# A state-space layer and a mixture of experts on one core: four states' products by TensorE in every sequence, and experts begun beside their second sequence's dispatch

## The chip, the cores and the metric

The kernel runs on one core of one Trainium2 chip. The metric is device time in microseconds (us) of one execution; lower is better. The engines have their usual names: TensorE (PE in the profile, with its weight loads as PEld), VectorE (DVE), ScalarE (ACT), GpSimd (POOL) and SyncE (SP), which here only issues DMAs.

## The reference

The input is 16 sequences of 512 positions and 256 channels, in float32. Two layers follow each other, each with a residual and a layer norm.

The first is a bidirectional selective state-space layer. A sequence is projected to 512 inner channels, convolved and gated. For each direction, with `u` (the convolved input), a step width `dt` per channel and position, and `B`, `C` per state and position (16 states), it computes

```
dA     = dt * A                                  # A negative, per channel and state
dB_u   = dt * u * B
dA_cum = exp(sum of dA over the later positions)
xs     = cumsum(dB_u * dA_cum) / (dA_cum + 1e-12)
y      = sum over states of xs * C  +  u * D
```

The two directions are added, gated and projected back to 256 channels.

The second is a soft mixture of 16 experts with 64 slots each. Logits of every position against 1024 slot embeddings are turned by a softmax over the positions into *dispatch* weights and by a softmax over the slots into *combine* weights. Each slot is the dispatch-weighted sum of a sequence's positions. Each expert applies `gelu(slots @ Wg + bg) * (slots @ Wu + bu) @ Wd + bd` to its slots, and the combine weights bring the results back to the positions.

## The kernel before

**The scan.** Sequences `b` = 0 to 15 run one after the other. A sequence has four parts (`scan_part`): direction `r` = 0 or 1, and half `p` of the channels (two blocks of 128 channels each). A part has 16 steps: for each pair of states `n, n+1` and each of the two blocks `c` there is one step, so a sequence has 64 steps and the kernel 1024. A step does, for the two states `j` = 0 and 1 of its block:

- GpSimd multiplies `du = dt * u` with the broadcast rows of `B`: `db` (L442), 128x1024 for both states.
- ScalarE computes the decay `exp(A * dt)` (L459), written into the PSUM tile `h`, and `th`, a tanh (L461) that stands for the division by `dA_cum + 1e-12`.
- VectorE runs the recurrence `h = h * decay + db` along the positions (L465 forward, L467 backward), and multiplies `(th + 1) * h` into `hg` (L470).
- GpSimd multiplies `hg` with the broadcast rows of `C` (L471).
- TensorE adds `hg` up over the states in the PSUM tile `acc` (L386, eight transposing matmuls). This is issued two steps later (`add_up(2)`).

For some states, TensorE makes `dt*u*B` in place of GpSimd (`by_diagonal`, L420): four matmuls of the transposed `du` (`duT`, L364) with a matrix that holds `B` on its diagonals (`dg`, loaded from DRAM) write the product into a PSUM tile `hd`. The step's `db` then has one state only (128x512), the decay of the other state goes into an SBUF tile `dec`, and the scan runs in place in `hd`. Which states is told by `diag_of`: 3, 7, 11 and 15 in sequences 0 to 2, and 5 and 13 from sequence 3 on. The matmuls for a step are issued after the step before it.

**PSUM.** Tiles `h` rotate through a pool of three banks (`ps_h`), `acc` through two, and everything else on TensorE through three shared banks (`bank()`, pool `ps`). In the kernel before, `hd` is one of the users of the shared banks. `diags` holds the number of each `hd` that is still waiting for its scan, so that no other user runs it over.

**What lies beside the scan.** Three lists of generators (`Side`) supply other work piece by piece. After each scan step, `beside_scan` calls on all of them:

- `prep`: the projections for the next part (`prep_forward`, `turn_back`, `prep_pair`, `turn_pair`), one piece per step.
- `front`: `finish` of the sequence before (transposes `pyt`, projection `po` L651, norm, `px2`) and its `dispatch` (logits `pl` L710, transposes `pd` L731, slots `pq` L746). Its 32 pieces are paced over the 64 steps.
- `back`: `experts` for a pair of sequences, in eight pairs of experts, each with the matmuls `pg` (L869, with the bias by L864), `pu` (L811) and `peo` (L838); and `combine` for each of the two sequences, with `cl` (L933), `ctp` (L954) and `cpo` (L1015) for each of four row blocks.

A piece ends with the matmuls into its banks; what reads the banks is issued at a later step (`HOLD`). A piece is begun only where the banks suffice. `paced_piece` gives a list its pieces: each step adds (pieces left) / (steps left) to a credit, and a piece takes 1.0 from it. Since all engines run their instructions in order, a piece on TensorE delays the `acc` and `hd` behind it, and a reader of it on VectorE or ScalarE delays the scans.

Experts of the sequences 2g and 2g+1 are put into `back` at the start of sequence 2g+3, when the dispatch of both is over, and with the two combines are spread over 128 steps, that is over an odd and the next even sequence. In effect the experts lie in the odd sequence and the combines in the even one. In the last sequence all that is left has 64 steps (`hurry`), and pieces marked `GAP` are no longer held off by a step. Experts and combine of the last two sequences follow after the scan, with more banks and buffers.

Of the kernel before, what the change touches and what calls it, by code (L numbers as in the profile page):

```python
# [9 lines left out]
F32 = mybir.dt.float32  # L10
# [7 lines left out]
P = 128  # L18
L = 512
# [36 lines left out]
def seq_layers(tc, ident, neghalf, a, out):  # L56
# [21 lines left out]
    nb = a["x"].shape[0]  # L78
    with ExitStack() as ctx:
# [17 lines left out]
        ps_h = scan_psum.enter_context(tc.tile_pool(name="m_h", bufs=3, space=PSUM))  # L97
# [7 lines left out]
        count = [0]  # L105

        def bank(name):
            count[0] += 1
            if tail and count[0] % 8 >= 3:
                return tail[0].tile([P, 512], F32, tag="tps", name=name)  # L110
            return ps.tile([P, 512], F32, tag="mps", name=name)
# [167 lines left out]

        def diag_of(b):  # L280

            return (3, 7, 11, 15) if b < 3 else (5, 13)

        def project_unit(b, r, out):

# [121 lines left out]
        def scan_part(b, r, p, v, accs, done, then):  # L407

            prep.drain()
            prep.gens += [[1, g] for g in [turn_pair(b, r, p, v)] + then]  # L410
            w, ds = side[r], diag_of(b)
            made = {}

            def by_diagonal(n, c):

                diags.append(count[0])
                made[n, c] = h = bank(f"hd_{b}_{r}_{n}_{c}")
                for lc in range(NL):
                    s = slice(lc * P, (lc + 1) * P)
                    ins = nc.tensor.matmul(h[:, s], v[c][3][:, s], dg[:, s], start=True, stop=True)  # L420
                    if lc == 0:
                        late(ins)

            chunks = (2 * p, 2 * p + 1)
            for n in range(0, NS, 2):
                q = f"{b}_{r}_{p}_{n}"
                k = 1 if n + 1 in ds else 2
# [11 lines left out]
                for c in chunks:  # L439
# [7 lines left out]
                    for j in range(2):  # L447
# [3 lines left out]
                        else:  # L451
                            h = made.pop((n + j, c))
# [4 lines left out]
                    for j in range(2) if k == 2 else (1, 0):  # L457
# [1 line left out]
                        nc.scalar.activation(hs[j][1], dt, AF.Exp, scale=w["A"][:, c, s])  # L459
                        ths[j] = p4.tile([P, L], F32, tag="th", name=f"th_{q}_{c}_{j}")  # L460
                        nc.scalar.activation(ths[j], rr, AF.Tanh, bias=LN_1E12 / 2, scale=w["Ah"][:, c, s])  # L461
                    for j in range(2):
                        (h, dec, add), th = hs[j], ths[j]
                        if r == 0:
                            nc.vector.tensor_tensor_scan(h, dec, add, 0.0, ALU.mult, ALU.add)  # L465
                        else:
                            nc.vector.tensor_tensor_scan(  # L467
                                h[:, ::-1], dec[:, ::-1], add[:, ::-1], 0.0, ALU.mult, ALU.add
                            )
                        nc.vector.scalar_tensor_tensor(hg[:, j, :], th, 1.0, h, ALU.add, ALU.mult)  # L470
# [5 lines left out]

                    nxt_n = n if c == chunks[0] else n + 2
                    if nxt_n + 1 in ds:
                        for x in sides:
                            x.take_up()  # L480
                        by_diagonal(nxt_n + 1, chunks[1] if c == chunks[0] else chunks[0])
                    beside_scan()
                    if k == 1:
                        diags.pop(0)
                    add_up(2)

        class Side:


            def __init__(self):  # L490
                self.gens, self.hold, self.need, self.left, self.credit = [], None, 0, 0, 0.0
                self.wait = self.took = self.gap = False

            def add(self, steps, gen):
                self.gens.append([steps, gen])

            def begin(self, scan_steps):
                self.left, self.credit = scan_steps, 0.0
# [20 lines left out]
            def piece(self, gaps=True):  # L519

                done = False
                while self.gens and self.hold is None and not self.wait:
                    if self.gap and self.took and gaps:
                        break
                    oldest = min([x.hold for x in sides if x.hold is not None] + diags[:1], default=count[0])
                    if count[0] - oldest + self.need > BANKS:
                        break
                    done = True
                    head = self.gens[0]
                    head[0] = max(head[0] - 1, 1)  # L530
                    fresh = len(head) == 2
                    if fresh:
                        head.append(True)
                    self.go()
                    if not fresh and (not self.gens or self.gens[0] is head):
                        break
                return done

            def paced_piece(self, gaps):
                self.credit = min(self.credit + sum(x[0] for x in self.gens) / max(self.left, 1), 2.0)  # L540
                self.left -= 1
                if self.credit >= 1.0 and self.piece(gaps):
                    self.credit -= 1.0

            def drain(self):
                while self.gens:
# [2 lines left out]
                    self.piece()  # L549

        hurry = False
        diags = []

        prep, front, back = sides = [Side(), Side(), Side()]

# [479 lines left out]
                yield WAIT  # L1035
                put(0, NL, *both)

        FINISH, COMBINE, PAIR = 32, 14, 4
        fwd = {}
        prep.add(1, prep_forward(0, 0, ND, fwd))  # L1040
        prep.drain()
# [6 lines left out]
        for b in range(nb):  # L1048
            bwd, nxt, accs = {}, {}, {}

            if b >= 3 and b % 2 == 1:
                g = (b - 3) // 2
                back.add(8 * PAIR, experts(g, 0, 8))
                back.add(COMBINE, combine(2 * g))
                back.add(COMBINE, combine(2 * g + 1))
            hurry = b + 1 == nb
            front.begin(64)
            back.begin(128 if b % 2 == 1 and b + 1 < nb else 64)

            def gate(c, b=b, accs=accs, bwd=bwd):  # L1060
                y = bwd["res"]
# [32 lines left out]
        g, kept = nb // 2 - 1, {}  # L1094
# [52 lines left out]
```

## Time and profile before

| What | us |
|---|---|
| median of three runs | 5326.35 (5323.48 to 5327.91) |
| the profiled execution | 5322.25 |
| its span in the profile | 5320.5 |
| sequence 2 (four states by TensorE, no back work) | 284.5 |
| sequence 3 (two states, experts) | 321.5 |
| sequence 8 (two states, combine) | 308.6 |
| sequence 9 (two states, experts) | 326.9 |
| sequence 14 (two states, combine) | 308.8 |
| sequence 15 (two states, experts and combine) | 372.6 |
| from the last scan step to the end | 240 |

A sequence is cut here at the end of every 64th product of L471. Sequences 4, 6, 10, 12 are within 1 us of sequence 8, and sequences 5, 7, 11, 13 within 1 us of sequence 9.

In a line of a group, the profile gives line, engine, operation, output<-inputs, shapes and count; then the busy time and the mean duration of one in ns; then the engine's idle time just before such instructions and what ended most of it. TensorE works on float32 here: one matmul of the program shows as two records in the profile, and a transposing one as one. In a line of a stretch the numbers after the length are the busy times of PE, PEld, DVE, ACT and POOL with their instruction counts, then the TensorE clock that was granted (1 is full), the DMA share and GB/s. In a line of waits: who waited for whom, total us, how often, the longest.

### The profile page before, as it was taken

Reading aid. Unit: us, or ns where it says so; the run is one execution under the profiler, and the core shown is the slowest. Engines: PE = TensorE matmul, PEld = TensorE weight load, DVE = VectorE, ACT = ScalarE, POOL = GpSimd, SP = SyncE. Lnnn points to the kernel's source line nnn. Section 1 sums busy time; section 2 is a strip of 40 time slices with the busy share of each in tenths; the row PEclk is TensorE's granted clock in tenths of the full one; section 3 lists DMA queues with packets and bytes.
Section 4 is the critical chain, followed back from the end, with each engine's and each line's share of the span. In section 5 each row is a group of like instructions: output and inputs, shape, how many; then the busy total and the mean of one; then the engine's idle time right before and its main releaser. Section 6 shows DMA issues by size and latency. Waiting matters only on the chain. (4 is left out here: it accounts for less than half of the span.)

```text
span 5320.5 us, 74550 instructions
## 1 busy us (share of the span) xinstructions
PE 4310.4 (81%) x24498; PEld 3411.1 (64%) x24498; DVE 4560.6 (86%) x6284; ACT 4104.9 (77%) x6573; POOL 4681.6 (88%) x2537
## 2 busy tenths in 40 slices
PE   5677776897778978788788878889787897878889
PEld 3556565676567756676666766667666676657667
DVE  7999999889998899888898888988898889987733
ACT  6777878887888877888887887888778887777644
POOL 6999999989999899999999989998999989988710
PEclk7778888998899989999899988899888998889999
DMA  5444444675446644576446754467544664447545
GB/s 141 137 129 152 126 142 131 211 234 152 146 146 224 222 144 143 171 226 206 132 140 198 236 169 151 134 210 230 157 151 144 217 227 149 144 153 230 168 135 168
DMA packets 614820, 907.82 MB, mean 171 GB/s; under 512 B 84606, under 2 KB 404734, under 8 KB 614432
## 3 DMA queue, kind: packets, MB, share of 16 engines
q1 hardware_dynamic: 532740, 859.35, 50.9%
q10 hardware_dynamic: 81692, 43.70, 3.1%
q8 instruction: 195, 3.19, 0.2%
q14 instruction: 193, 1.58, 0.1%
HBM read 840.34 MB, written 62.56 MB: 170 GB/s over the span
## 5 line engine op out<-in xcount | busy, mean ns | idle before, releaser
L471 POOL TENSOR_TENSOR hg<-hg,cs 128x1024 f32<-128x1024 f32 x1024 | 2416.9, 2364 | 125.0 <-DVE hg L470 108.0
L442 POOL TENSOR_TENSOR db<-du,bs 128x1024 f32<-128x1024 f32 (+1 forms) x1024 | 2087.7, 2042 | 227.8 <-DVE h L465 84.1
L470 DVE SCALAR_TENSOR_TENSOR hg<-th,h 128x512 f32<-128x512 f32 x1744 | 1156.8, 679 | 183.4 <-PE acc L386 105.9
L386 PE MATMUL acc<-ident,hg 128*128 128x128 f32 x8192 | 1163.6, 292 | 106.4 <-POOL hg L471 84.6
L386 PEld LDWEIGHTS acc<-ident,hg 128*128 128x128 f32 x8192 | 1034.4, 152 | 284.6 <-POOL hg L471 131.3
L467 DVE TENSOR_TENSOR_SCAN h<-h,db 128x512 f32<-128x512 f32 x872 | 1044.9, 1219 | 104.9 <-ACT h L459 92.6
L465 DVE TENSOR_TENSOR_SCAN h<-h,db 128x512 f32<-128x512 f32 x872 | 1044.1, 1219 | 44.5 <-ACT h L459 43.6
L461 ACT ACTIVATE th<-rr,Ah_f 128x512 f32<-128x512 f32 x1024 | 724.6, 714 | 200.9 <-DVE hg L470 198.1
L461 ACT ACTIVATE th<-rr,Ah_b 128x512 f32<-128x512 f32 x1024 | 721.3, 712 | 153.5 <-DVE hg L470 143.5
L459 ACT ACTIVATE h<-dt,A_f 128x512 f32<-128x512 f32 x872 | 591.4, 680 | 99.5 <-DVE hg L470 96.3
L459 ACT ACTIVATE h<-dt,A_b 128x512 f32<-128x512 f32 x872 | 592.3, 680 | 85.6 <-DVE hg L470 81.7
L420 PE MATMUL hd<-dg,duT 128*128 128x128 f32 x2432 | 375.7, 305 | 73.2 <-ACT duT L364 27.1
L420 PEld LDWEIGHTS hd<-dg,duT 128*128 128x128 f32 x2432 | 347.9, 220 | 84.5 <-ACT duT L364 29.5
L710 PE MATMUL pl<-x2T,seT 128*128 128x512 f32 x512 | 294.1, 704 | 78.4 <-DVE hg L470 37.4
L838 PE MATMUL peo<-Wd,ht 128*128 128x256 f32 x1024 | 258.1, 408 | 63.2 <-DVE rr L346 36.6
L869 PEld LDWEIGHTS pg<-st,Wg 128*128 128x128 f32 x2048 | 243.1, 195 | 94.1 <-issue 82.8
L811 PE MATMUL pu<-st,Wu 128*128 128x128 f32 x2048 | 255.6, 284 | 49.3 <-DMA Wu<-in_Wu_dram 27.0
L1015 PE MATMUL cpo<-ceo,ct 128*128 128x256 f32 x1024 | 256.0, 407 | 43.2 <-DVE rr L346 40.0
L811 PEld LDWEIGHTS pu<-st,Wu 128*128 128x128 f32 x2048 | 245.9, 199 | 60.6 <-DVE h L467 29.5
L838 PEld LDWEIGHTS peo<-Wd,ht 128*128 128x128 f32 x1024 | 205.5, 206 | 106.1 <-DVE rr L346 39.2
L869 PE MATMUL pg<-st,Wg 128*128 128x128 f32 x2048 | 265.0, 284 | 4.5 <-DMA st<-s_dram 3.4
L1015 PEld LDWEIGHTS cpo<-ceo,ct 128*128 128x128 f32 x1024 | 207.2, 207 | 87.2 <-DVE rr L346 42.7
(165 smaller groups left out, 6754.0 us busy)
## 6 DMA issues: line engine op xcount, KB each, us to landing
cs<-bc SPq DMA_DIRECT2D x512, 512.0 KB, 3.9
bs<-bc SPq DMA_DIRECT2D x360, 512.0 KB, 5.2
Wg<-in_Wg_dram SPq DMA_DIRECT2D x128, 512.0 KB, 5.7
Wu<-in_Wu_dram SPq DMA_DIRECT2D x128, 512.0 KB, 5.8
Wd<-in_Wd_dram SPq DMA_DIRECT2D x128, 512.0 KB, 5.5
dg<-diag_dram SPq DMA_DIRECT2D x152, 256.0 KB, 4.3
bs<-bc SPq DMA_DIRECT2D x152, 256.0 KB, 3.5
x<-in_x_dram SPq DMA_DIRECT2D x32, 512.0 KB, 6.5
```

The costliest lines, as they stand in the source:

```text
L386: ins = nc.tensor.matmul(accs[c][:, s], hc[:, j, s], ident, is_transpose=True, start=False, stop=(last and j == 1 and lc == NL - 1),)
L420: ins = nc.tensor.matmul(h[:, s], v[c][3][:, s], dg[:, s], start=True, stop=True)
L442: nc.gpsimd.tensor_tensor(db[:, :k, :], du.unsqueeze(1).to_broadcast([P, k, L]), bs[:, :k, :], ALU.mult)
L459: nc.scalar.activation(hs[j][1], dt, AF.Exp, scale=w["A"][:, c, s])
L461: nc.scalar.activation(ths[j], rr, AF.Tanh, bias=LN_1E12 / 2, scale=w["Ah"][:, c, s])
L465: nc.vector.tensor_tensor_scan(h, dec, add, 0.0, ALU.mult, ALU.add)
L467: nc.vector.tensor_tensor_scan(h[:, ::-1], dec[:, ::-1], add[:, ::-1], 0.0, ALU.mult, ALU.add)
L470: nc.vector.scalar_tensor_tensor(hg[:, j, :], th, 1.0, h, ALU.add, ALU.mult)
L471: nc.gpsimd.tensor_tensor(hg, hg, cs, ALU.mult)
L811: nc.tensor.matmul(pu[:, fc * P : (fc + 1) * P], got["Wu", e][:, k, fc * P : (fc + 1) * P], st[:, k, :, j * SL : (j + 1) * SL], start=(k = ...
L838: nc.tensor.matmul(po[:, j * DM : (j + 1) * DM], ht[:, fc, :], got["Wd", e0 + j][:, fc, :], start=(fc == 0), stop=(fc == NF - 1),)
L869: nc.tensor.matmul(pg[:, fc * P : (fc + 1) * P], got["Wg", e][:, k, fc * P : (fc + 1) * P], st[:, k, :, j * SL : (j + 1) * SL], start=(not ...
```

## The change

- `diag_of` gives the states 3, 7, 11 and 15 in every sequence.
- `hd` is taken from the scan's own three banks (`ps_h`, tag `h`) and not from the shared ones; the list `diags` and its place in the limit of `piece` go. In a step with an `hd`, VectorE runs the scan of `hd` first. Before an `hd` is made, only `prep` is taken up, and not `front` and `back`.
- Experts of the sequences 2g and 2g+1 are put into `back` at the start of sequence 2g+2. The first of them wait (`ready`) until the dispatch of sequence 2g+1, which runs beside that same sequence, has stored their slots; in the changed program's order of instructions that is after half of the sequence. The pace of `back` is a constant 0.5 credits per step; a piece of experts takes 1.1, one of combine 0.8. Only the last sequence keeps a pace by what is left.

```diff
         def diag_of(b):
 
-            return (3, 7, 11, 15) if b < 3 else (5, 13)
+            return (3, 7, 11, 15)
...
             prep.drain()
-            prep.gens += [[1, g] for g in [turn_pair(b, r, p, v)] + then]
+            prep.gens += [[1, g, 1.0] for g in [turn_pair(b, r, p, v)] + then]
...
             def by_diagonal(n, c):
 
-                diags.append(count[0])
-                made[n, c] = h = bank(f"hd_{b}_{r}_{n}_{c}")
+                made[n, c] = h = ps_h.tile([P, L], F32, tag="h", name=f"hd_{b}_{r}_{n}_{c}")
...
-                    for j in range(2):
+                    for j in range(2) if k == 2 else (1, 0):
                         (h, dec, add), th = hs[j], ths[j]
...
                     if nxt_n + 1 in ds:
-                        for x in sides:
-                            x.take_up()
+                        prep.take_up()
                         by_diagonal(nxt_n + 1, chunks[1] if c == chunks[0] else chunks[0])
                     beside_scan()
-                    if k == 1:
-                        diags.pop(0)
                     add_up(2)
...
             def __init__(self):
+                self.rate = None
...
-            def add(self, steps, gen):
-                self.gens.append([steps, gen])
+            def add(self, pieces, gen, weight=1.0):
+                self.gens.append([pieces, gen, weight])
...
-                    oldest = min([x.hold for x in sides if x.hold is not None] + diags[:1], default=count[0])
+                    oldest = min([x.hold for x in sides if x.hold is not None], default=count[0])
...
-                    fresh = len(head) == 2
+                    fresh = len(head) == 3
...
             def paced_piece(self, gaps):
-                self.credit = min(self.credit + sum(x[0] for x in self.gens) / max(self.left, 1), 2.0)
+                rate = self.rate or sum(x[0] for x in self.gens) / max(self.left, 1)
+                self.credit = min(self.credit + rate, 2.0)
                 self.left -= 1
+                weight = self.gens[0][2] if self.gens else 0.0
                 if self.credit >= 1.0 and self.piece(gaps):
-                    self.credit -= 1.0
+                    self.credit -= weight
...
-        FINISH, COMBINE, PAIR = 32, 14, 4
+        FINISH, COMBINE, EXPERTS = 32, (13, 0.8), (25, 1.1)
+        back.rate = 0.5
...
-            if b >= 3 and b % 2 == 1:
-                g = (b - 3) // 2
-                back.add(8 * PAIR, experts(g, 0, 8))
-                back.add(COMBINE, combine(2 * g))
-                back.add(COMBINE, combine(2 * g + 1))
+            if b >= 2 and b % 2 == 0:
+                g = b // 2 - 1
+                back.add(EXPERTS[0], experts(g, 0, 8), EXPERTS[1])
+                for i in range(2):
+                    back.add(COMBINE[0], combine(2 * g + i), COMBINE[1])
             hurry = b + 1 == nb
             front.begin(64)
-            back.begin(128 if b % 2 == 1 and b + 1 < nb else 64)
+            if hurry:
+                back.rate = None
+                back.begin(64)
```

The matmuls per half sequence (32 steps) in the two programs' order of instructions, for an even sequence and the odd one after it (hd, pairs of experts begun with pg, row blocks begun with cl, blocks of pl):

| Half | before: hd, pg, cl, pl | after: hd, pg, cl, pl |
|---|---|---|
| even, first | 8, 0, 4, 2 | 16, 0, 1, 3 |
| even, second | 8, 0, 4, 6 | 16, 5, 0, 5 |
| odd, first | 8, 4, 0, 2 | 16, 3, 2, 3 |
| odd, second | 8, 4, 0, 6 | 16, 0, 5, 5 |

More of the change, by code (lines that the diff above doesn't have):

```diff
@@ L551, in seq_layers @@
         hurry = False
-        diags = []
         prep, front, back = sides = [Side(), Side(), Side()]
```

## The prediction

> **What bounds the kernel now.** I read the page for totals, then cut the run at every 64th L471 product (64 scan steps are one sequence) and asked for the busy time in those stretches, then in half sequences, and last for the waits in one half. Engine totals:
>
> ```profile
> PE 4310.4 (81%) x24498; PEld 3411.1 (64%) x24498; DVE 4560.6 (86%) x6284; ACT 4104.9 (77%) x6573; POOL 4681.6 (88%) x2537
> ```
>
> and, of the groups by form (operation, shapes, count, busy us, mean ns, idle before and what ended it):
>
> ```profile
> L442 POOL TENSOR_TENSOR db<-du,bs 128x1024 f32<-128x1024 f32 x720 | 1699.9, 2366 | 181.2 <-issue 70.2 <-DVE h L465 56.5 <-DVE h L467 42.0
> L442 POOL TENSOR_TENSOR db<-du,bs 128x512 f32<-128x512 f32 x304 | 387.9, 1277 | 46.7 <-DVE h L465 27.5 <-POOL hg L471 11.2 <-DMA bs<-bc 4.2
> L420 PE MATMUL hd<-dg,duT 128*128 128x128 f32 x2432 | 375.7, 305 | 73.2 <-ACT duT L364 27.1 <-ACT yt L645 13.6 <-DMA dg<-diag_dram 10.2
> L465 DVE TENSOR_TENSOR_SCAN hd<-dec,hd 128x512 f32<-128x512 f32 x152 | 184.9, 1217 | 25.8 <-PE hd L420 21.1 <-ACT h L459 4.7
> L467 DVE TENSOR_TENSOR_SCAN hd<-dec,hd 128x512 f32<-128x512 f32 x152 | 184.8, 1215 | 42.9 <-PE hd L420 40.6 <-ACT th L461 2.1
> ```
>
> No engine is full over the whole run, so the stages decide. Sequences 2 (four states, no experts), 8 (combine), 9 (experts), 15 (the last), and the end; the columns are stretch, length, busy PE, PEld, DVE, ACT, POOL, then the granted clock:
>
> ```profile
> 618.00:902.50 284.50, 202.81 (x1169) 164.38 (x1167) 262.78 (x325) 227.90 (x364) 276.70 (x154) 0.83 0.43 136
> 2493.70:2802.30 308.60, 246.07 (x1284) 186.60 (x1283) 282.88 (x385) 247.87 (x415) 295.09 (x157) 0.88 0.44 140
> 2802.30:3129.20 326.90, 283.56 (x1740) 230.75 (x1739) 283.95 (x397) 262.17 (x399) 295.20 (x157) 0.94 0.67 214
> 4707.50:5080.10 372.60, 313.84 (x1842) 251.86 (x1841) 285.07 (x416) 265.38 (x416) 287.92 (x151) 0.93 0.59 187
> 5080.10:5320.00 239.90, 216.77 (x1216) 177.29 (x1214) 71.71 (x199) 97.36 (x210) 14.68 (x44) 0.97 0.52 160
> ```
>
> GpSimd bounds the first two (97% and 96% busy). In sequence 9 nothing is over 91%, yet it takes 18.3 us more than 8 with the same GpSimd work. Its halves, with the first half of 2 and the second of 8 and 15, show why:
>
> ```profile
> 618.00:761.20 143.20, 102.51 (x603) 84.23 (x602) 131.81 (x165) 112.24 (x181) 139.46 (x82) 0.82 0.44 135
> 2648.40:2802.30 153.90, 126.42 (x635) 92.77 (x635) 140.48 (x194) 124.59 (x209) 146.87 (x77) 0.91 0.45 141
> 2802.30:2966.00 163.70, 133.92 (x844) 112.62 (x842) 140.27 (x195) 131.29 (x200) 150.09 (x85) 0.92 0.65 206
> 2966.00:3129.20 163.20, 149.64 (x896) 118.13 (x897) 143.68 (x203) 130.88 (x200) 145.11 (x73) 0.97 0.69 222
> 4894.50:5080.10 185.60, 159.13 (x898) 125.50 (x897) 141.46 (x209) 125.75 (x211) 137.73 (x68) 0.95 0.53 167
> ```
>
> Where experts lie beside dispatch (2966 to 3129) TensorE is 92% busy at a clock of 0.97, and the waits there run from it to VectorE and on to GpSimd:
>
> ```profile
> DVE hg L470 <- PE acc L386: 9.4, 9, 2.4
> DVE nm L715 <- PE pl L710: 3.3, 3, 1.7
> DVE hd L467 <- PE hd L420: 3.0, 3, 1.9
> ...
> POOL hg L471 <- DVE hg L470: 9.4, 4, 5.2
> POOL db L442 <- DVE h L465: 5.3, 2, 3.0
> ```
>
> So the even sequences are GpSimd's, the second half of the odd ones TensorE's. The change takes from the first and gives to the second.
>
> **The change part by part.** (1) *Two more states on TensorE in sequences 3 to 15*: 13 x 2 directions x 4 blocks x 2 = 208 more hd. GpSimd: 208 x (2366 - 1277 ns) = 226 us less, 17.4 us a sequence, 8.7 a half. TensorE: 375.7 / 304 = 1.24 us each, 257 us more, 9.9 a half. VectorE: nothing, the scan reads hd in 1215 to 1217 ns. ScalarE: each decay goes to the buffer dec in 713 instead of 680 ns, 7 us in all under an engine 77% busy. SyncE: 104 more dg loads, with as many bs loads halved, so the bytes stay; sequences 1 and 2 issue as many and wait little. I take nothing.
>
> (2) *hd in the scan's own three buffers, its scan first.* The front and back pieces get the shared banks to themselves. An hd now needs the multiply (L470) three tiles earlier, the last of the step before last; matching the timeline of sequence 9 to the order of instructions, 15 of 16 hd began after that, so the buffer costs nothing there. VectorE, in order, now reaches hd one scan and one multiply (1.22 + 0.68 = 1.9 us) sooner, and behind that wait stand the multiplies that GpSimd needs. In sequence 9, 12 of the 16 hd ended 1.1 to 5.4 us after VectorE had finished the step before. But there VectorE was waiting for acc four steps back, that is for the same TensorE, so waiting earlier need not add. Ends: -3 us a sequence (the whole 3.7 us of waits for hd is gone) and 16 x 1.9 = 30 us an expert half. I take 0, nearest to sequence 2, which runs all 32 with 0.6 us of such waits.
>
> (3) *Experts start one sequence earlier, at 0.5 credits a step.* I count pieces in the changed program's order. One pair of experts costs TensorE 265.0/64 + 128.4/56 (pg and its bias) + 255.6/64 (pu) + 258.1/64 (peo) = 14.5 us; one row block of combine 3.8 (cl) + 1.3 (ctp) + 4.0 (cpo) = 9.1 us; a pl pair 2.3.
> - Even, first half: like the first half of sequence 2, plus a last combine block or two: 143.2 + 2 = 145.
> - Even, second half: five pairs beside dispatch. Against 2966 to 3129: one pg and one pu more (10.4), a pl pair less (2.3), eight hd more (9.9): TensorE 149.6 + 18 = 167.7. Ends: nothing more if TensorE had room, 163; at the same 92%, 182. I take 97%, 173: the stretch is already TensorE's, and the freed banks should remove some of its idle.
> - Odd, first half: against 2802 to 2966 one pg and pu less (10.4), two cl, a ctp and a pl pair more (11.2), eight hd (9.9): TensorE 133.9 + 10.7 = 144.6, GpSimd 150 - 9. Ends 155 (all that GpSimd gives) and 174 (all that TensorE adds). I take 162, close to no change.
> - Odd, second half: combine beside dispatch, as in the second half of 8, with a cl, two ctp and a cpo more (10.3), a pl pair less and eight hd: TensorE 126.4 + 17.9 = 144.3, GpSimd 138, VectorE about 143. Ends 145 and 172; I take 151, as GpSimd was the limit.
>
> A pair is then 145 + 173 + 162 + 151 = 631, against 308.6 + 326.9 = 635.5: -4.5. The first pair of experts also reads slots just written: s_dram lands in 3.9 us and st in 4.2, and pg is four steps (some 18 us) behind the last product for them. I take 0; uncovered it is 8.1 us x 7 with acc queued behind.
>
> Sum: sequence 2 gets experts, 143 + 173 - 284.5 = +32. Sequence 3 took 321.5: 313 - 321.5 = -8. Pairs 4 to 13: 5 x -4.5 = -23. Sequence 14 has one pg more: 322 - 308.8 = +13. Sequence 15: first half 154.7 of TensorE becomes 152.6, 187 to 184; second half loses two pg and three pu and peo, gains seven hd, 159 - 31 = 128, like the second half of 8 (153.9) but with the gaps rule off: 160, so -28 in all. The end: three combine blocks (27 us of TensorE) are gone from the 48 us (5084 to 5132) before the first pl of the end, where TensorE is busy for 41.6 us and the chain runs pyt, po, moments, px; -18, ends 0 and -27. Together -32 on the profiled execution's 5322.25 us; the median shown is 4.1 above it, so **5294**.
>
> The Trainium skill's page "Perfetto Trace Analysis" (section Identifying the Most-Contended Engine) says that TensorE's matmul busy share is no measure of its headroom and that the weight loads' share should be taken. Here PEld is 118.13 of 163.20, 72%, which would leave room for all that is added and give the sum of the first rival; the waits on acc in the same stretch speak against it, so I keep the 92%.
>
> **The rivals.** *TensorE has room, GpSimd was the limit everywhere.* For: GpSimd is at 89 to 92% even in sequence 9. Against: there it waits for VectorE, not the reverse. Pair: 143 + 163 + 155 + 147 = 608, -27.5. Sum: +22 - 19 - 137 - 2 - 40 - 20 = -196, 5130.
>
> *Slower: VectorE waits for hd.* Place: L465/L467 of hd in the expert halves, 14 of them with 16 each, 224. For: late hd in sequence 9 as above, 61.7 us of such waits already with hd second, 0.2 us each. Price: 224 x 0.47 us = 105, 5400; the other end is 224 x 1.9 = 426. It decides from 0.14 us each, where my 32 us are eaten.
>
> *Nothing comes of it.* What GpSimd loses TensorE takes, pairs at 635 to 638, the end and sequence 15 paying for sequence 2: within 0.2% of 5326.
>
> **How the numbers follow.** Forecast 0.45 (its own range 5250 to 5340, from 167 to 180 for the seven even second halves), room on TensorE 0.16, waits for hd 0.28, nothing 0.11. The range 5180 to 5400 leaves out somewhat over half of the first rival, whose mild form lies between it and the forecast, and a third of the second. Within 0.2% (10.7 us, about what a measurement here can tell) lie most of the last case and a little of the forecast: 0.10. Faster: 0.16 + 0.40 of the forecast = 0.56. Slower: 0.34.
>
> **What would show it.** GpSimd's busy time down to about 4455 us and TensorE's up to some 4550. Even and odd sequences near 318 and 313 us, sequence 2 at 316, sequence 15 near 345, the end near 222. Even second halves with TensorE at 95% or over show the binding step right; 163 us there shows the first rival. Waits of hd's scan for L419 over 100 us, with the expert halves beyond 180 us, show the second. The forecast is wrong above all if the even second half is: 5 us there are 35 us in all, more than the whole gain.

## The result: slower by 1.8%

The changed kernel takes 5423.43 us (median of four runs, 5420.05 to 5424.19) against 5326.94 of the kernel before beside it: a ratio of 1.0181, 95% interval [1.0163, 1.0199]. The forecast was 5294, that is faster, in a range of 5180 to 5400. The profiled execution took 5420.05, its span 5418.2. Totals of the page after:

```profile
PE 4437.0 (82%) x26162; PEld 3567.8 (66%) x26162; DVE 4561.7 (84%) x6284; ACT 4125.7 (76%) x6583; POOL 4469.1 (82%) x2537
```

GpSimd lost the busy time that it should lose (4681.6 to 4469.1), and no other engine filled up in its place: VectorE, now the fullest at 84%, is as busy as before. VectorE, ScalarE and GpSimd stand idle longer (760 to 857, 1216 to 1293 and 639 to 949 us); TensorE does not (1010 to 981). Groups by form after (x512 of the short `db`, 512 hd):

```profile
L441 POOL TENSOR_TENSOR db<-du,bs 128x1024 f32<-128x1024 f32 x512 | 1212.2, 2368 | 314.1 <-DVE h L466 103.0 <-DVE h L464 80.8 <-issue 79.5
...
L441 POOL TENSOR_TENSOR db<-du,bs 128x512 f32<-128x512 f32 x512 | 653.6, 1277 | 281.9 <-DVE h L464 200.1 <-DVE h L466 74.3 <-DMA bs<-bc 4.4
...
L419 PE MATMUL hd<-dg,duT 128*128 128x128 f32 x4096 | 621.5, 301 | 171.5 <-ACT duT L364 64.9 <-issue 54.3 <-DVE hg L469 43.4
...
L466 DVE TENSOR_TENSOR_SCAN hd<-dec,hd 128x512 f32<-128x512 f32 x256 | 312.0, 1219 | 117.5 <-PE hd L419 116.6 <-ACT th L460 0.8
...
L464 DVE TENSOR_TENSOR_SCAN hd<-dec,hd 128x512 f32<-128x512 f32 x256 | 311.4, 1217 | 108.6 <-PE hd L419 108.6
```

The durations are the ones forecast. What grew is the idle time: GpSimd's before `db` from 228 us to 596, three quarters of it (458) for VectorE's scans, and VectorE's for hd from 62 us to 225 (0.44 us for each of 512, 0.20 before).

The first half of sequence 8 before, for the table below:

```profile
2493.70:2648.40 154.70, 119.65 (x651) 93.83 (x649) 142.40 (x192) 123.28 (x207) 148.22 (x81) 0.86 0.44 139
```

The stretches after, in order: first half of sequence 2; the four halves of 8 and 9; the halves of 15; the end.

```profile
631.00:781.20 150.20, 103.02 (x603) 86.80 (x603) 130.84 (x164) 111.42 (x179) 139.67 (x82) 0.82 0.41 129
2578.20:2733.70 155.50, 117.00 (x675) 99.27 (x676) 139.65 (x183) 120.80 (x200) 141.68 (x85) 0.85 0.44 139
2733.70:2906.60 172.90, 157.77 (x980) 127.35 (x981) 141.53 (x200) 134.74 (x200) 137.09 (x73) 0.96 0.70 217
2906.60:3072.30 165.70, 139.75 (x880) 113.95 (x879) 145.49 (x203) 132.95 (x206) 140.27 (x82) 0.96 0.64 194
3072.30:3226.10 153.80, 131.84 (x742) 98.61 (x740) 140.91 (x198) 126.09 (x213) 138.53 (x76) 0.98 0.45 142
4862.00:5044.30 182.30, 153.77 (x926) 123.92 (x923) 145.88 (x208) 130.11 (x205) 140.30 (x81) 0.93 0.57 176
5044.30:5201.20 156.90, 128.24 (x730) 103.38 (x730) 129.67 (x186) 112.34 (x198) 130.18 (x67) 0.92 0.34 110
5201.20:5418.00 216.80, 189.23 (x1089) 157.27 (x1088) 63.41 (x177) 90.11 (x192) 14.62 (x45) 0.96 0.57 175
```

| Stretch | before | forecast | after |
|---|---|---|---|
| sequences 0, 1 | 277.2, 283.3 | the same | 283.4, 290.4 |
| sequences 2, 3 | 284.5, 321.5 | 316, 313 | 323.1, 319.5 |
| even, first half | 154.8 | 145 | 156.2 |
| even, second half | 153.6 | 173 | 174.7 |
| odd, first half | 163.8 | 162 | 165.7 |
| odd, second half | 162.8 | 151 | 155.0 |
| sequence 14 | 308.8 | 322 | 331.1 |
| sequence 15 | 372.6 | 345 | 339.2 |
| the end | 240 | 222 | 217 |

(Halves: means over sequences 4 to 14 and 5 to 13. Sequence 0 is counted from the start of its first L471 product, L470 after.) The even second half, on which the forecast was said to hang, came out 2 us from it. The even first half did not get shorter at all, though GpSimd has 7 us less to do there. Over the run, sequences 0 to 3 are 27 us above the forecast, the five pairs from 4 to 13 are 651.5 us each in place of 631 (+102), 14 is +9, 15 and the end -11: together 127 of the 130 us between 5290 (forecast for a profiled execution) and 5420.

The longest waits that grew, after and then before (who waited for whom, total us, times, longest):

```profile
ACT h L458 <- DVE hg L469: 379.4, 396, 4.1
...
PE pd L729 <- ACT et L725: 161.1, 45, 7.4
...
DVE hd L466 <- PE hd L419: 116.6, 73, 5.6
DVE hd L464 <- PE hd L419: 108.6, 55, 7.9
...
ACT dec L458 <- DVE hd L466: 82.7, 78, 4.3
...
ACT dec L458 <- DVE hd L464: 53.5, 58, 2.9
...
PE hd L419 <- DVE hg L469: 43.4, 32, 4.8
```

```profile
ACT h L459 <- DVE hg L470: 178.0, 183, 5.1
...
PE pd L731 <- ACT et L727: 62.1, 23, 6.0
...
ACT dec L459 <- DVE hd L465: 20.3, 27, 3.0
...
ACT dec L459 <- DVE hd L467: 14.2, 22, 1.0
...
PE hd L420 <- DVE hg L470: 3.9, 5, 1.6
```

ScalarE's decays wait twice as long for the multiply that frees a scan bank, and those in `dec`, which has two buffers, four times as long for the scan of an earlier hd (34.5 to 136.2 us). TensorE stands longer at `pd`, the reader of ScalarE's `et`, and waits itself for a free scan bank (43.4 us for 3.9). The hd in TensorE's queue behind these comes late to VectorE. That `et` is late because the decays before it in ScalarE's queue had waited is read from the order of the queue and not shown: of the 161 us at `pd`, ScalarE stands for that multiply in only 10, and is busy with `et`, `h` and `th` in 109.

### The profile page after: what moved, and what is told of

It is laid out like the page before. It is cut to its first block, busy times and chain, and to the rows that moved or that the text cites. A ratio compares the mean times of both kernels' runs of the same rounds, so it can differ in the third digit from the quotient of the medians.

```text
span 5418.2 us, 78150 instructions
## 1 busy us (share of the span) xinstructions
PE 4437.0 (82%) x26162; PEld 3567.8 (66%) x26162; DVE 4561.7 (84%) x6284; ACT 4125.7 (76%) x6583; POOL 4469.1 (82%) x2537
## 5 line engine op out<-in xcount | busy, mean ns | idle before, releaser
L470 POOL TENSOR_TENSOR hg<-hg,cs 128x1024 f32<-128x1024 f32 x1024 | 2421.5, 2365 | 99.6 <-DVE hg L469 88.0
L441 POOL TENSOR_TENSOR db<-du,bs 128x1024 f32<-128x1024 f32 (+1 forms) x1024 | 1865.9, 1822 | 596.0 <-DVE h L464 280.9
L469 DVE SCALAR_TENSOR_TENSOR hg<-th,h 128x512 f32<-128x512 f32 x1536 | 1017.2, 677 | 131.0 <-PE acc L386 64.1
L466 DVE TENSOR_TENSOR_SCAN h<-h,db 128x512 f32<-128x512 f32 x768 | 923.2, 1218 | 98.4 <-ACT h L458 96.4
L464 DVE TENSOR_TENSOR_SCAN h<-h,db 128x512 f32<-128x512 f32 x768 | 919.8, 1215 | 67.8 <-ACT h L458 65.7
L419 PE MATMUL hd<-dg,duT 128*128 128x128 f32 x4096 | 621.5, 301 | 171.5 <-ACT duT L364 64.9
L419 PEld LDWEIGHTS hd<-dg,duT 128*128 128x128 f32 x4096 | 568.1, 214 | 227.6 <-ACT duT L364 98.8
L458 ACT ACTIVATE h<-dt,A_f 128x512 f32<-128x512 f32 x768 | 525.9, 686 | 222.0 <-DVE hg L469 213.9
L458 ACT ACTIVATE h<-dt,A_b 128x512 f32<-128x512 f32 x768 | 521.7, 682 | 179.1 <-DVE hg L469 165.5
L466 DVE TENSOR_TENSOR_SCAN hd<-dec,hd 128x512 f32<-128x512 f32 x256 | 312.0, 1219 | 117.5 <-PE hd L419 116.6
L464 DVE TENSOR_TENSOR_SCAN hd<-dec,hd 128x512 f32<-128x512 f32 x256 | 311.4, 1217 | 108.6 <-PE hd L419 108.6
L469 DVE SCALAR_TENSOR_TENSOR hg<-th,hd 128x512 f32<-128x512 f32 x512 | 346.1, 676 | 48.7 <-ACT th L460 33.6
L809 PEld LDWEIGHTS pu<-st,Wu 128*128 128x128 f32 x2048 | 263.6, 211 | 66.6 <-ACT th L460 43.4
L931 PE MATMUL cl<-seT,cx 128*128 128x512 f32 x480 | 240.6, 644 | 52.9 <-ACT xb L258 26.5
```

The source lines that it names most:

```text
L441: nc.gpsimd.tensor_tensor(db[:, :k, :], du.unsqueeze(1).to_broadcast([P, k, L]), bs[:, :k, :], ALU.mult)
L466: nc.vector.tensor_tensor_scan(h[:, ::-1], dec[:, ::-1], add[:, ::-1], 0.0, ALU.mult, ALU.add)
L470: nc.gpsimd.tensor_tensor(hg, hg, cs, ALU.mult)
L809: nc.tensor.matmul(pu[:, fc * P : (fc + 1) * P], got["Wu", e][:, k, fc * P : (fc + 1) * P], st[:, k, :, j * SL : (j + 1) * SL], start=(k = ...
```

## The experiments

Eighteen runs. Each time is a median, with the ratio to the kernel before run beside it, and the difference from that (the later expectations took 5326.94 or so for all, and have 201, 97 and 47 us for what is 202, 94 and 45 here). Steps of the prediction: (2) is hd in the scan's banks, with all that goes with it; (3) is the schedule.

### One part at a time

**Step (2) alone**: two states from sequence 3 on, old schedule.

```diff
-made[n, c] = h = bank(f"hd_{b}_{r}_{n}_{c}")      # and diags, its brake in `piece`
+made[n, c] = h = ps_h.tile([P, L], F32, tag="h", ...)
-for j in range(2):
+for j in range(2) if k == 2 else (1, 0):
-for x in sides: x.take_up()
+prep.take_up()
```

> hd in the scan's own banks with its scan first; states and experts' schedule as in the kernel before (304 hd). Theory A (the banks and the order of the scans make VectorE wait for hd): sequences 0 and 1, which differ from before in this alone, took 6.2 and 7.1 us more in the changed kernel, 32 hd each, 0.21 us per hd; so 304 x 0.21 = 63 us slower, about 5390, and waits of hd's scan for the matmul well above the 62 us of before. Theory B (the added matmuls under experts load TensorE too much): 13 us slower from sequences 0 and 1 only, about 5340.

5528.82, 1.0377 [1.0359, 1.0394]: **+202 us**. ScalarE's waits for the multiply are 474 us, VectorE's for hd 197, TensorE's at `pd` 154.

**Step (3) alone**: only the pieces' weights, `back.rate = 0.5`, and experts a sequence earlier; hd in the shared banks, two states.

> Experts started at the even sequences at 0.5 credits a step; two states from sequence 3 on and shared banks as before. Theory A: the schedule is not the cause, and the relief of sequence 15 (-33 us) and of the end (-23 us) pays for sequence 2 (+30) and 14 (+13): 5300 to 5330. Theory C (experts beside dispatch at the denser pace make the loss): pairs of sequences 15 us slower, 5400 or more.

5536.09, 1.0398 [1.0378, 1.0417]: **+209**. The even halves take 166 and 173 us, the odd ones 173 and 165 (means as above); sequence 15 gives 39 us back and the end 12.

**States and banks**, the old schedule (step (2) with four states everywhere).

> Four states in all sequences, own banks, scan of hd first; experts' schedule as before (begun at the odd sequences over 128 steps). Theory A: even sequences (combine) gain what GpSimd gives and lose 32 x 0.21 us, near 308 as before; odd ones (experts) get slower, 335; 5380 to 5430. Theory C: back near 5327 or below, as the schedule made the loss.

5489.48, 1.0305 [1.029, 1.0321]: **+162**.

**Banks and schedule**, with two states from sequence 3 on.

> Own banks and the new schedule, but two states from sequence 3 on (304 hd): the third path between before and after. If the parts add (banks +201, states -39, schedule -66): 5423 + 39 = 5462. If the states pay only under the new schedule, or the schedule only with four states: 5500 or more. Below 5423: the added states are a cost after all.

5582.05, 1.0483 [1.0458, 1.0508]: **+254**. So the parts do not add. With (2) in place, the two further states are worth 39 us under the old schedule (5529 to 5489) and 159 under the new one (5582 to 5423); the schedule costs 53 with two states and brings 66 with four. The changed kernel with its hd in the shared banks throughout was not run, so what step (2) costs inside the full change has no run of its own.

### What in step (2) costs

**The pool alone**: hd from `ps_h`, but counted as a user of a shared bank, so that the brake, the taking up and the order of the scans stay.

```diff
-made[n, c] = h = bank(f"hd_{b}_{r}_{n}_{c}")
+count[0] += 1
+made[n, c] = h = ps_h.tile([P, L], F32, tag="h", ...)
```

> The kernel before, with hd moved to the scan's own three banks and nothing else: the limit that holds pieces off while an hd waits (the brake), the taking up of all lists ahead of an hd, and the order of the scans stay. The whole set of bank edits cost 201 us with the states and schedule of before. Theory A2 (an hd in the scan's banks leaves ScalarE's decays without a bank; ScalarE in order then holds up everything behind them): most of it is here, 5450 or more, and ScalarE's waits of h for the multiply rise from 178 us to 400 or more. Theory A3 (without brake and early taking up, pieces stand on TensorE ahead of hd and acc and wait there for ScalarE): 5320 to 5350, waits of pd for et stay near 62 us.

5423.58, 1.0175 [1.0159, 1.019]: **+94**, from one edit that leaves the durations of scans and products as they were (1210 to 1218, 2363, 2365 and 1277 ns). Its waits:

```profile
ACT h L460 <- DVE hg L471: 414.5, 406, 6.2
...
PE pd L732 <- ACT et L728: 145.1, 47, 11.6
...
PE hd L421 <- DVE hg L471: 72.7, 56, 3.5
...
DVE hd L468 <- PE hd L421: 71.1, 37, 8.2
...
DVE hd L466 <- PE hd L421: 41.8, 20, 4.4
```

These are the waits above, now with one cause, the pool: 178 to 414 us, 62 to 145, 3.9 to 72.7, and VectorE's waits for hd from 62 to 113. How much of the 94 us comes by `et` and how much by TensorE's own waits for a scan bank was not separated. The three banks of `ps_h` let ScalarE make decays up to three tiles ahead. An hd takes one of them while it is made and until it is multiplied. The second halves pay: 162.8 to 172 in the odd sequences, 4 to 6 us in the even ones from 4 on, +7 to +12 in sequences 0 to 2. The even first halves from 4 on pay nothing (153 to 155).

**prep alone taken up**, all else as before.

> The kernel before, but only prep is taken up ahead of an hd; banks and brake as before. A2: within 20 us of 5327. A3: a good part of the 201 us, 5380 or more, with waits of pd for et above 100 us.

5374.07, 1.0083 [1.0068, 1.0098]: **+45**. **The opposite**, step (2) with all three lists taken up:

> All bank edits on the kernel before (own banks, no brake, hd first) but all lists taken up ahead of an hd, as before. If the parts of the 201 us add (banks with brake 97, early taking up 47, the rest 57): 5529 - 47 = 5482. If the missing brake is what matters: 5500 or more. If the late taking up is most of it: below 5450.

5467.69, 1.026 [1.0245, 1.0276]: +140, so late taking up is 61 of the 202. It seemed a fixed price, to be had back in the changed kernel too. The same line in the changed kernel, and in states and banks under the old schedule:

> The changed kernel with one line back as it was: ahead of an hd all three lists are taken up, not prep alone. With two states and the old schedule that line was worth 61 us (5529 to 5468). Theory A, the late readers of front and back pieces hold PSUM banks and fall due between a step's scans whatever the states and schedule: 50 to 70 us less than 5423, so 5353 to 5373, with VectorE's waits for hd down from 225 to some 150 us. Theory B, with four states and constant pace the pieces are spread well enough, and an hd behind the readers comes later: 5410 to 5440, waits for hd unchanged or up.

> Four states in all sequences, hd in the scan's banks, the old schedule, all lists taken up ahead of an hd. It stands to the run with prep alone taken up (5489) as one line. Theory A (the line costs 61 us anywhere): 5420 to 5440. Theory B (the line matters with two states only, since with four there is an hd before every second step and the lists are taken up often either way): 5480 to 5500.

5584.29, 1.0482 [1.0465, 1.05], and 5537.9, 1.04 [1.0384, 1.0415]: 161 and 48 us *worse* than with prep alone. Theory A was wrong, and B too by its size. With two states the line saves 45 or 61 us, with four it costs 48 or 161. In the odd second halves of the first of the two, 155 us became 179. One of them, in the stretch and then in TensorE's waits:

```profile
3167.40:3346.20 178.80, 151.04 (x784) 113.32 (x782) 147.15 (x209) 130.57 (x222) 138.90 (x77) 0.90 0.40 124
```

```profile
PE ctp L953 <- ACT cm L946: 11.2, 2, 6.7
```

TensorE has 6% more records than in 3072 to 3226 of the changed kernel (784 for 742; 32 of the 42 are one block of combine) and is busy for 15% longer, at a granted clock of 0.90 against 0.98. It stood twice for `cm`, where in the changed kernel this wait is 1.4 us.

**The order of the two scans**: the changed kernel with the line `for j in range(2)` as before.

> The changed kernel, but in a step with an hd VectorE scans the other state first, as before. Theory A1 (it is the order: VectorE reaches hd 1.9 us too early): sequences 0 and 1 go back to 277 and 283, waits of hd's scan from 225 us to under 100, 5330 or below. Theory A2 (it is the banks: hd may not be made until the multiply three tiles before, and the decays may not run ahead): 5400 to 5430, the waits move from hd's scan to others.

5424.89, 1.0183 [1.0168, 1.0198]: nothing. The 1.9 us that the prediction weighed are not where the loss is.

### Taking the bank shortage away

**The other state's h in SBUF** in steps with an hd, in the free half of `db`.

```diff
-dec = h = ps_h.tile([P, L], F32, tag="h", ...)
+dec = h = ps_h.tile(...) if k == 2 else db[:, 1, :]
```

> The changed kernel, but in a step with an hd the other state's h lies in the free half of its SBUF tile db and not in a PSUM bank, so such a step takes one of the three banks as before and not two. A2: ScalarE's waits of h for the multiply fall from 379 us to some 200, hd's scan waits less than 150 of 225 us, 5300 to 5360. A3: no change of these, 5410 or more (slower by what a scan with both inputs in SBUF costs).

6063.42, 1.1372 [1.1355, 1.1389]. ScalarE's waits for the multiply fell from 379 to 166 us and VectorE's for hd from 225 to 50, as the bank theory said. The loss is another: groups by form,

```profile
L473 POOL TENSOR_TENSOR hg<-hg,cs 128x1024 f32<-128x1024 f32 x1024 | 2605.4, 2546 | 598.2 <-DVE hg L472 389.4 <-issue 80.3 <-DVE sm L727 19.4
...
L472 DVE SCALAR_TENSOR_TENSOR hg<-th,db 128x512 f32<-128x512 f32 x512 | 776.7, 1517 | 72.6 <-PE acc L386 33.5 <-ACT xd L302 24.0 <-ACT th L463 5.1
...
L469 DVE TENSOR_TENSOR_SCAN db<-db 128x512 f32<-128x512 f32 x256 | 559.7, 2193 | 13.9 <-ACT db L461 13.9
...
L467 DVE TENSOR_TENSOR_SCAN db<-db 128x512 f32<-128x512 f32 x256 | 537.2, 2103 | 6.6 <-ACT db L461 6.6
```

With both inputs in SBUF, VectorE's scan takes 2103 to 2193 ns (1215 to 1219 with one in PSUM) and its multiply 1517 (677); GpSimd's product goes from 2365 to 2546. In the same trace the 26 such scans with no GpSimd instruction beside them take 1204 ns on average, the 163 such multiplies 679, and GpSimd's products beside neither 2360: it is the overlap that costs. The Trainium skill's page "SBUF — State Buffer" (section Who interferes with whom) states that a DVE instruction with two SBUF inputs contends with a GpSimd instruction that reads SBUF; these numbers agree.

**Four banks for the scan**, two shared.

```diff
-ps_h: bufs=3,  ps: bufs=3,  BANKS = 3
+ps_h: bufs=4,  ps: bufs=2,  BANKS = 2
```

> The changed kernel with four banks for h and hd and two shared ones. A2: sequences 0 and 1, where the shared banks are little used, return to 277 and 284 us; in all 5300 to 5420, as the pieces lose a bank. A3: sequences 0 and 1 stay at 283 and 290, in all 5430 or more.

5740.55, 1.0771 [1.0753, 1.0789]. ScalarE's waits for the multiply are gone, but VectorE's for hd are 305 us and those of `dec` for an earlier hd 225; that the pieces starve on two banks is likely and not shown. One thing it tells: the first halves of sequences 0 and 1 stay at 145 and 148 (147 and 149 in the changed kernel), so there the shortage of scan banks seems to be 1 to 2 of the 6 us, unless the shared bank that is missing here hides more.

### The first sequences, and the load of TensorE

In sequence 0, with the same states and no back work, the first half lost 6 us. VectorE's waits there, before and after:

```profile
DVE hd L467 <- PE hd L420: 2.8, 4, 1.8
```

```profile
DVE hd L464 <- PE hd L419: 9.0, 4, 7.8
DVE hd L466 <- PE hd L419: 4.0, 2, 3.3
```

Without the brake a piece of prep (`px`, L291) is ahead of the hd of the state 7 in TensorE's order; it stands there for ScalarE's `xb`, and hd behind it.

**Sequences 0 and 1 with hd as before, and a pace of 0.375**: two edits in different stretches.

```diff
+hd, brake, taking up and order of scans as before if b < 2
-back.rate = 0.5
+back.rate = 0.375
```

> The changed kernel with two edits that act in different stretches. In sequences 0 and 1 hd lies in the shared banks as before, with the brake, the taking up of all lists and the old order of scans. From sequence 2 on the pace of back is 0.375 credits a step in place of 0.5, so that in the order of instructions the even second half begins 4 pairs of experts in place of 5, the odd halves 3 and 1 in place of 3 and 0, and the even first half 4 blocks of combine in place of 1. First edit, theory A (the order of pieces around hd costs the first halves there): first halves of sequences 0 and 1 back to 141 and 143 from 147.0 and 149.3, 12 us in all; rival: unchanged, the loss being in later work. Second edit, theory A (the even second half is TensorE's at 175 and the even first half, with TensorE busy 116 of 156 at a granted clock of 0.85, has room): even 158 to 160 and 162 to 165, odd 164 and 157, a pair 641 to 646 in place of 652, so 36 to 66 us less over six pairs, 5345 to 5375 for the whole with the first edit. Rival B (a piece costs its TensorE time wherever it lies): a pair of 650 to 654, 5405 to 5415 for the whole. Rival C (the blocks of combine in the even first half take banks and stall hd as in the old schedule, 165): a pair above 655, 5430 or more.

5440.14, 1.0209 [1.0191, 1.0226]. First edit: first halves 139.9 and 143.1 us, theory A within about a microsecond. So step (2) as a whole, without any other change of work, costs 6 to 7 us in each first half there. Which part of it: with the old order of scans these halves stay at 146.1 and 150.6, with all lists taken up at 146.6 and 147.6, with four scan banks at 145.1 and 148.3; with the pool alone, under the brake, they are 142.2 and 145.1. That points to the missing brake, so to the place of the pieces, though no run takes the brake alone. Second edit, in the halves of 8 and 9:

```profile
2567.00:2738.80 171.80, 134.00 (x737) 105.74 (x738) 142.59 (x203) 125.65 (x213) 141.56 (x85) 0.86 0.42 127
2738.80:2907.10 168.30, 141.99 (x850) 112.75 (x848) 142.43 (x193) 132.12 (x203) 138.66 (x78) 0.94 0.62 195
2907.10:3076.60 169.50, 141.86 (x914) 120.54 (x914) 140.62 (x198) 129.84 (x196) 140.25 (x81) 0.90 0.64 198
3076.60:3233.30 156.70, 136.10 (x774) 106.49 (x774) 138.63 (x188) 124.59 (x204) 136.98 (x73) 0.96 0.53 159
```

Here the even second half gets lighter and 5 us shorter, and the even first half, with three blocks of combine more, 16 us longer, though TensorE is busy for only 134 of 171.8. Sequence 8 is the extreme: the means of the four halves are 165.5, 162.3, 171.5 and 158.2, so +9 for the even first half and -12 for the even second one, and a pair is 657.5 against 651.5. By the number that is theory C, not A; its mechanism is not shown by it.

**hd made twice**: each of the four matmuls issued a second time over the first, from sequence 3 on.

> The changed kernel with each of the four matmuls of an hd issued twice from sequence 3 on, the second over the first: 416 x 1.2 = 500 us more of TensorE, 20 us a half sequence, nothing more for any other engine. Theory A (only the even second half is TensorE's, as the forecast had it at 173 of which 167.7 busy; it measured 175 with 160 busy): even second +17 to +20, the others, with TensorE busy 116, 140 and 132, less than half of it, +5 to +9, partly since the granted clock rises; 5423 + 6 x (19 + 22) + some 20 = about 5690. Theory B (the order on TensorE counts, not its load: VectorE stands on hd, which comes 1.2 us later by its own making, 16 times a half): every half +15 to +20 alike, 5423 + 26 x 18 = about 5890. Theory C (TensorE has room, its stalls come from others): even second +5 or less, 5500 at most.

5580.67, 1.0465 [1.0448, 1.0483], 157 more than the changed kernel (152 when each is taken against the kernel before beside it), less than A and B expected. Halves of 8 and 9:

```profile
2638.90:2793.50 154.60, 124.99 (x802) 107.59 (x802) 139.38 (x184) 121.35 (x199) 141.50 (x85) 0.90 0.45 140
2793.50:2978.50 185.00, 171.48 (x1114) 142.57 (x1113) 142.50 (x201) 137.54 (x204) 137.13 (x73) 0.96 0.65 203
2978.50:3147.20 168.70, 149.99 (x992) 127.24 (x991) 143.70 (x200) 131.18 (x201) 140.15 (x81) 0.96 0.65 190
3147.20:3311.60 164.40, 147.45 (x882) 115.03 (x881) 143.37 (x199) 128.15 (x216) 138.91 (x78) 0.99 0.43 133
```

Sixteen hd twice cost 12.1, 3.0 and 10.6 us in the last three, and in the even first half -0.9. There TensorE does more (125 for 117 us), hd comes later by its own making, the clock goes from 0.85 to 0.90, and the time stays. So the even first half is not TensorE's, by load or by the length of an hd, unless the higher clock happens to make up for both. The even second half is TensorE's, as forecast, and the odd second one, forecast as GpSimd's, answers to it almost as much.

### Fewer states, and the last experts

The kernel before with four states in even sequences, with three (5, 9, 13) from sequence 3 on, and with three in even sequences from 4 on; hd in the shared banks.

> The kernel before, with four states on TensorE in the even sequences too (which GpSimd bounds, 96% busy, and where no experts lie), hd in the shared banks, everything else as before; 96 hd more. If GpSimd's work is worth there what it was in sequence 2 (284.5 us with 97% busy): even sequences from 308.5 to about 298, 5265. If hd on the shared banks holds up front and back as it does in the scan's banks: 5330 or more.

> The kernel before, with states 5, 9, 13 in place of 5, 13 from sequence 3 on, hd in the shared banks, all else as before. GpSimd loses 104 x 1.09 = 113 us, TensorE gains 129. Theory A (each further hd in the shared banks holds pieces back and bunches them; four states in the seven even sequences, 112 hd, cost 140 us): about 5326 + 130 = 5456. Theory B (the third state still fits between the pieces, only the fourth did not): 5290 to 5330.

> The kernel before, with states 5, 9, 13 in the even sequences from 4 on, two in the odd ones. 48 hd more beside combine alone. Theory A (bunching by the shared banks): 48 of the 112 hd that cost 140 us, so +60, 5386. Theory B (GpSimd bounds the even sequences at 96% busy, and a little relief there is worth what GpSimd loses, 8.7 us a sequence in six sequences): 5326 - 40 = 5286.

5468.17, 1.0258 [1.0243, 1.0273]; 5516.0, 1.0352 [1.0337, 1.0368]; 5454.92, 1.0242 [1.0224, 1.0259]. None gains. The brake that protects an hd seems to hold the pieces back until they bunch: in the first of these, steps 8 to 15 of sequence 8 have TensorE busy for 45.1 of 46.3 us, against 30.0 of 39.1 in the kernel before. With three states from sequence 3 on, 346 us are left for the end in place of 240, 106 of the 188 lost; while the pieces are put off, the first halves of sequences 3 and 5 take 151.5 and 157.2 in place of 159.2 and 163.8.

The kernel before with the experts of sequences 12 and 13 begun at sequence 14:

> The kernel before, with only the experts of sequences 12 and 13 begun at sequence 14 and not 15 (spread over 128 steps). From the changed kernel, sequence 15 and the end gain 33 and 23 us and sequence 14 loses 13 to 22: 5290 to 5310. If the relief needs the four states: 5327 or more.

5339.68, 1.0022 [1.0012, 1.0031]: sequence 14 loses 14 us, 15 gains 2.3, and the end loses 2.4. No run beat the kernel before.

## Why the prediction was wrong

**Step (1), the states: right in size.** GpSimd's busy time was to be 4455 and is 4469; hd's own TensorE time rose by 246 us (forecast 257), the scan stayed at 1217 to 1219 ns, the decay in `dec` takes 714. TensorE's total was to be 4550 and is 4437: what lies beside took 119 us less in sum (a matmul of `pl` 615 ns for 704, one of `pu` 296 for 284), which goes with less time at half clock (below).

**Step (2) failed: "the buffer costs nothing there", "I take 0".** Its ends were -3 us a sequence and +30 us an expert half, and the value was taken from sequence 2 with its 0.6 us of waits. That row shows hd in the *shared* banks with the brake and all lists taken up, which is what the edit removes. The pool alone costs 94 us, the whole step 202 with two states under the old schedule. I weighed only whether hd would be late by the order of the two scans (worth nothing) and whether its bank is free when it starts. The latter was read from a timeline with hd elsewhere and did not hold: TensorE waits 43.4 us for that multiply in the changed kernel, 72.7 with the pool alone, 3.9 before. And I did not ask whom hd keeps out of that bank: ScalarE's decays, which then wait for the multiply 379 us in place of 178, or 414 with the pool alone. What step (2) is worth inside the full change can't be given as one number, since the parts interact (step (3) alone costs 209 us, and (1) to (3) together 97); in sequences 0 and 1, where nothing else changes, restoring its old form brings the whole 13 us back. There the runs point less to the bank than to the brake that the step takes away.

**Step (3): three of four halves near, the even first one wrong.** 173, 162 and 151 were 174.7, 165.7 and 155.0; "even, first half: like the first half of sequence 2, 143.2 + 2 = 145" was 156.2, 11 of the 20.5 us by which a pair is over. Of these 11, 7 are in the base: sequence 2's own first half takes 150.2 after, with TensorE busy 103.0 for 102.5 and GpSimd alike, which is step (2) again: with step (2) alone that half is 150.2 too. The other 4 come with the work that was costed at 2: a combine row block or two and three blocks of `pl` for two. The doubled hd speak against TensorE's load. That it is the place of these pieces and of their readers, as in sequence 0, is argued and not shown.

The small terms held: the first experts' reads of slots just written cost 4.0 us in all (3.4 before), sequence 15 and the end came out 6 and 5 us below their forecasts. "TensorE at 95% or over" did not show: 91% at 174.7 us, so the time was right and its share not: 167.7 us of TensorE were added up and 157 to 162 were there, and two misses met in 173. That is luck in part. So it is with the odd second half, whose 151 rested on GpSimd as the limit: it is within 4 us, but sixteen hd made twice lengthen it by 10.6.

**The rivals.** "VectorE waits for hd" named the wait that grew most on VectorE: the 225 us are 163 more than before, and its price, 5400, lies nearest to what was measured. Its place is hit in part only. The 14 expert halves (even second and odd first) hold 130 of the 225 us, yet from sequence 4 to 14 they came out 2 and 4 us above the forecast, none before sequence 15 took over 180, and with each hd's own matmuls doubled the even first half lost nothing. "TensorE has room" is excluded: the even second half is 174.7, not 163, and answers to TensorE work. The Trainium skill's page "Perfetto Trace Analysis" (section Identifying the Most-Contended Engine) judges TensorE's headroom by MFU and the weight loads' share, not by matmul busy time. That share does not tell the stretches apart here: PEld is 64% in the even first half of sequence 8 and in the odd second one of 9 alike, and the doubled hd cost -0.9 and +10.6 us.

## What to carry to other kernels

Before giving a bank of a rotating pool to a new user, ask who gets it later, and follow that engine's queue in order to the next engine that waits for it; a row that shows the new user cheap in its old place says nothing of this. Where several lists share in-order engines, a halt or a taking up of lists is worth something only for one arrangement: the same line, taking up all lists, was worth 45 and 61 us with two states and cost 48 and 161 with four. Price a moved step against a stretch that has the move already, and if there is none, let the range hold the full cost.

## What was not expected of the hardware

The granted TensorE clock in these records is either 1 or 0.5, and every stretch at 0.5 but the last is a whole multiple of 3.41 us (in the changed kernel 79 of one, 40 of two, 23 of three). Before has 174 stretches at 0.5, 1100 us together, the changed kernel 150 and 906, the pool alone 206 and 1261, and the changed kernel with all lists taken up 188 and 1209. The changed kernel, with more for TensorE to do, has less time at half clock than before, which fits TensorE's busy time rising by 127 us where hd alone added 246. With all lists taken up, TensorE is idle for 1065 us in place of 981, and the time at half clock comes back. By the matmul records of the changed kernel, TensorE is busy for 25% of the 3.4 us before a drop to 0.5 (mean of 148), and for 98% of the last 3.4 us before the return to 1 (never under 79%). The Trainium skill's page "TensorE: Matmul & The Clock Gate" (section Part 1: The HAM clock gate) has the throttled state as the default, released by activity and returning after an idle window. The records agree that the clock follows TensorE's activity, but the stretches before a drop are not idle ones here.

How much of each loss is the clock and how much the waiting that brings it about was not separated.
